# Setting constants of q and k on GpSimd instead of ScalarE, and loading the square-root table first, at the start of a gated attention kernel

## The chip, the core and the metric

The kernel runs on one core of one Trainium2 chip. The metric is the device time of one execution in microseconds. Three runs of the kernel before gave 3406.14 us as their median (3406.01 to 3406.58).

## What is computed

All data are float32. `x` has shape (2, 2048, 256). The reference, cut to what matters:

```
x = L0_attn_x
xn = layernorm(x)
s  = attn(xn)            # 16 heads of 16, over all 2048 tokens, with a spatial bias on a
                         # 256 x 256 corner of the scores; then W_proj, + b_proj, + layernorm(xn)*gamma+beta
g  = silu(ffn(xn))       # two layers: windowed attention with rotary positions, then a gated MLP
out = x + s * g

attn: qkv = xn @ W_qkv.T;  a = softmax(q @ k.T * hd**-0.5 + bias);  (a @ v) @ W_proj.T
```

The change lies in the first attention, `attn`, and there in its beginning.

## The kernel before

**Stages.** `global_attention` computes `s` in units of (batch element, group of 4 heads, 512 queries). In each it first finds the largest score of every query (`max_piece`, L364 on VectorE over L361's products), then forms the scores again with the maximum taken off (L397), their exponentials (L403 on ScalarE) and the sums with v (L416). `ffn_branch` follows. The change and the prediction concern the first 130 us or so, before the exponentials begin.

**The beginning.** x of batch element 0 is loaded in four chunks of 512 tokens (L226, four DMAs of 512 KB on SyncE's queue). For each chunk VectorE takes mean and variance (L212, L213), ScalarE takes the root (L234), VectorE the reciprocal and a shift (L235, L237), ScalarE scales the chunk in four pieces (L244), TensorE transposes it (L257) and ScalarE copies it to `xA` (L258). Then TensorE projects it to k and q (L293) and v (L327). k and q go by way of DRAM (L300 out, L308 back), because each head of 16 rows has to stand in a strip of 32 rows. `both` interleaves the lists of such steps of neighbouring chunks; this order is written out by hand, and every engine executes its own list in order. `spatial_bias` is interleaved later: ScalarE L100, L101, VectorE L102, ScalarE L103, three times.

**Constant places.** In the strip of 32 rows of a head, row 16 of `kT` holds ones and row 16 of `qT` takes the negative maximum later (`augment`); the other rows above 15 do not matter as long as those of `qT` are zero. `v` holds a one beside each head's 16 columns. There are two buffers of each, for alternating groups. `set_rest(i)` sets buffer i whole, before the DMAs of L308 write the 16 rows of each head: `kT` from `ones_col`, a column with a one in row 16 of each strip of 32, and `qT` from a zero column, both on ScalarE; `v` by a memset on GpSimd. It is called once at the head of the step lists and once for buffer 1 after the four chunks, ahead of the bias.

**What sets the order.** Up to `tc.manual_schedule()` a scheduler decides the order of an engine's instructions from the dependences; behind it the order is the program's. DMAs of SyncE's and ScalarE's queues take eight completion semaphores in rotation, in scheduler order. If the semaphore that a DMA is to take is still out, the DMA's issue waits until the earlier user has landed, and the queue behind it waits too. In the built program this gives, for the first DMAs (SyncE's in brackets): vecs 0, (x chunk 0) 1, b2 2, ones_col 3, wk 4, (x chunk 1) 5, wk 6, wq 7, (x chunk 2) 0, wq 1, wv 2, (x chunk 3) 3, wv 4, gam 5, bet 6, bpr 7. So x chunk 2 waits for vecs, x chunk 3 for ones_col, the second wv for the first wk, gam for x chunk 1, bet for the second wk, bpr for the first wq. ScalarE's DMA issues stand ahead of its first compute instruction.

The weights wk, wq, wv arrive padded (L161) and are packed on GpSimd (L164), each in two halves. `wp` is loaded by sixteen DMAs on GpSimd's own queue (L195).

Of the kernel before, what the change touches and what calls it, by code (L numbers as in the profile page):

```python
# [11 lines left out]
F32 = mybir.dt.float32  # L12
AF = mybir.ActivationFunctionType
ALU = mybir.AluOpType
AX = mybir.AxisListType
PSUM = bass.MemoryType.PSUM

B, N, D = 2, 2048, 256
P = 128
NT = N // P  # L20
# [6 lines left out]
NG, GH, HD, HP = 4, 4, 16, 32  # L27
NPR, PH = 2, 8
VW = HD + 1
VALL = (PH - 1) * VW + HP  # L30
# [10 lines left out]
def gated_recurrent_kernel(ctx: ExitStack, tc: tile.TileContext, t: dict, out: bass.AP):  # L41
# [31 lines left out]

    s_all = [s_pool.tile([P, NT, D], F32, tag=f"s{b}", name=f"s{b}") for b in range(B)]
    global_attention(tc, t, xA, s_all, s_out, ident, eps_t, x_ch, early)
    ffn_branch(tc, t, xA, s_out, weights, ident, eps_t, mean_w, vecs, b2_row, x_ch, out_ch)

# [59 lines left out]
def global_attention(tc, t, xA, s_all, s_out, ident, eps_t, x_ch, early):  # L137
# [9 lines left out]
    nc = tc.nc  # L147
    with ExitStack() as ctx:
        cp = ctx.enter_context(tc.tile_pool(name="ga_c", bufs=1))
        p2 = ctx.enter_context(tc.tile_pool(name="ga_2", bufs=2))  # L150
        psr = ctx.enter_context(tc.tile_pool(name="ps_r", bufs=1, space=PSUM))

        ones_col = cp.tile([P, 1], F32, name="ones_col")
        nc.scalar.dma_start(ones_col, t["ones"][:, 2 * P :])

        w, padded = {}, {}
        for n in ("wk", "wq", "wv"):
# [4 lines left out]
                padded[n, k] = x  # L162
        for n, k in padded:
            nc.gpsimd.tensor_copy(w[n][:, k].rearrange("p (h d) -> p h d", d=HD), padded[n, k][:, :, :HD])  # L164

        qTs = [cp.tile([P, N], F32, name=f"qT{i}") for i in range(2)]
        kTs = [cp.tile([P, N], F32, name=f"kT{i}") for i in range(2)]
        vs = [cp.tile([P, NT, VALL], F32, name=f"v{i}") for i in range(2)]
        zero = xA[0][:, 0, 0:1]

        def set_rest(i):
            nc.scalar.copy(kTs[i], ones_col.to_broadcast([P, N]))
            nc.scalar.copy(qTs[i], zero.to_broadcast([P, N]))
            nc.gpsimd.memset(vs[i], 1.0)

        dram = ctx.enter_context(tc.tile_pool(name="qk_d", bufs=1, space=bass.MemoryType.DRAM))
        qk_d = {}
# [170 lines left out]
        def max_piece(j):  # L348
            n, at = divmod(taken[j], TPC * NCH)
            if n >= len(units):  # L350
                return
            taken[j] += 1
            i, c = divmod(at, NCH) if n else divmod(at, TPC)[::-1]
            b, g, qc = units[n]
            qT, kT, _ = qkv[b * NG + g]
            if n not in mxs:
                mxs[n] = p2.tile([P, TPC * GH, NCH], F32, tag="mx", name=f"mx_{n}")
            rows = slice(j * HP, (j + 1) * HP)
            ps = bank(f"pm_{n}_{i}_{c}_{j}", ring="p")
            q0 = qc * CH + i * P  # L360
            nc.tensor.matmul(  # L361
                ps, qT[rows, q0 : q0 + P], kT[rows, c * CH : (c + 1) * CH], start=True, stop=True
            )
            nc.vector.tensor_reduce(mxs[n][:, i * GH + j, c : c + 1], ps, AX.X, ALU.max)  # L364
            if all(x >= (n + 1) * TPC * NCH for x in taken):
                nc.vector.tensor_reduce(negm[n % 2][:, :, HD : HD + 1], mxs[n], AX.X, ALU.max, negate=True)
                others.insert(0, lambda: augment(n))
# [122 lines left out]
        def both(a, b):  # L490

            n = max(len(a), len(b))
            for i in range(n):
                for x in (a, b):
                    for f in x[i * len(x) // n : (i + 1) * len(x) // n]:
                        f()
# [2 lines left out]
        turns = [firsts[c][0][3:] + firsts[c][1] for c in range(NCH)]  # L499
        preps = [first_preps(c) for c in range(NCH)]  # L500
        maxima = [[(lambda j=j: max_piece(j)) for _ in range(TPC) for j in range(GH)] for _ in range(NCH + 1)]
        set_rest(0)
        both(stat[0], [])
        both(turns[0], stat[1])
        both(preps[0] + turns[1], stat[2])
        both(preps[1] + turns[2], stat[3])
        both(maxima[0], preps[2] + turns[3])
        both(maxima[1], preps[3])
        set_rest(1)
        rest = [lambda: next(sb) for _ in range(4)] + prep[3 * NCH :]  # L510
        both(maxima[2] + maxima[3], rest[:-4])
        both(maxima[4][: LEAD * GH], [lambda: others.pop(0)()] + rest[-4:])
# [689 lines left out]
```

## Time and profile before

| | |
|---|---|
| median of three runs | 3406.14 us |
| the profiled execution's own time | 3405.59 us |
| its span, first to last instruction | 3403.8 us |
| mean granted TensorE clock | 0.987 |
| GpSimd: first / last packing copy of the weights | 9.72 / 15.59 us |
| GpSimd: the sixteen wp issues | 16.93 to 24.93 us |
| GpSimd: two memsets of v | 24.92 to about 29.0 us |
| first L361 of the maxima | 43.63 us |
| first exponential's table load | 133.95 us |

The profile shows one execution. A line of its timeline gives start and length in us, engine, line of the kernel, operation, result<-operands, how many were merged, and in brackets how long the engine stood idle before and what released it. ACTq, SPq and POOLq are the instruction queues' DMA issues, PEld is TensorE's weight load. In the 40 slices a digit is the busy share in tenths.

### The profile page before, as it was taken

The numbers are of one execution on the slowest core, as the hardware profiler recorded it, in microseconds if no ns is written. First come the engines' busy times: TensorE is split into PE (matmuls) and PEld (weight loads), VectorE is DVE, ScalarE is ACT, GpSimd is POOL, SyncE is SP. The second block draws the span as 40 slices with busy tenths as digits, with TensorE's granted clock in tenths as the row PEclk, the third lists the DMA queues.
The fourth block names the chain that finished last, engine by engine and source line by source line (L and its number), as shares of the span: only waits on it lengthen the run. The fifth ranks groups of instructions, "written<-read, shape, count | busy, mean of one in ns | idle before, by whom it ended". The sixth has DMA issues, their size and how long they took to land. (4 is left out here: it accounts for less than half of the span.)

```text
span 3403.8 us, 55360 instructions
## 1 busy us (share of the span) xinstructions
PE 3325.0 (98%) x21280; PEld 1631.7 (48%) x21280; DVE 2314.9 (68%) x4978; ACT 2092.9 (61%) x4237; POOL 1105.2 (32%) x949
## 2 busy tenths in 40 slices
PE   6999999999999999999999799999999999999999
PEld 3444444444444444444444355555555555666565
DVE  3798889877777787787775366666666666665642
ACT  3477676667776677767677576555555555555542
POOL 2012111111111111111111455555555555655631
PEclk8899999999999999999999899999999999999999
DMA  2100000000000100000000100000000000000001
GB/s 93 51 1 6 21 1 14 14 14 14 7 18 21 46 14 1 4 10 1 1 7 7 62 9 1 7 1 7 1 25 8 1 17 25 10 19 19 20 19 49
DMA packets 39768, 56.78 MB, mean 17 GB/s; under 512 B 8830, under 2 KB 24274, under 8 KB 39506
## 3 DMA queue, kind: packets, MB, share of 16 engines
q1 hardware_dynamic: 37266, 50.88, 4.7%
q8 instruction: 168, 2.75, 0.3%
q10 hardware_dynamic: 1728, 2.12, 0.2%
q14 instruction: 94, 0.77, 0.1%
q0 software_dynamic: 512, 0.26, 0.0%
HBM read 36.45 MB, written 16.78 MB: 16 GB/s over the span
## 5 line engine op out<-in xcount | busy, mean ns | idle before, releaser
L364 DVE TENSOR_REDUCE mx<-pm 128x1 f32<-128x512 f32 x2048 | 1272.2, 682 | 357.1 <-PE ps L397 311.7
L403 ACT ACTIVATE e<-ps 128x512 f32<-128x512 f32 x2048 | 1069.7, 602 | 258.2 <-PE ps L397 179.0
L361 PE MATMUL pm<-kT,qT 32*128 32x512 f32 x4096 | 1166.2, 626 | 3.6 <-DVE mx L364 3.6
L397 PE MATMUL ps<-qa,kT 32*128 32x512 f32 x4096 | 1109.6, 625 | 14.1 <-ACT e L403 14.1
L427 POOL TENSOR_TENSOR o<-o,part 128x512 f32<-128x512 f32 x224 | 284.3, 1269 | 1449.6 <-ACT part L426 1439.3
L361 PEld LDWEIGHTS pm<-kT,qT 32*128 32x128 f32 x4096 | 486.7, 185 | 375.3 <-DVE mx L364 262.6
L397 PEld LDWEIGHTS ps<-qa,kT 32*128 32x128 f32 x4096 | 442.1, 184 | 212.1 <-ACT e L403 142.5
L416 PE MATMUL po<-e,v 128*32 128x512 f32 x4096 | 497.5, 604 | 1.7 <-DVE mx L364 1.7
L721 PE MATMUL pp<-weights,xA 128*128 128x512 f32 x768 | 361.6, 606 | 0.8 <-DVE s L471 0.8
L937 PE MATMUL pg<-hc,weights 128*128 128x512 f32 (+1 forms) x768 | 357.6, 596 | 1.1 <-DVE hc L918 1.1
L743 POOL TENSOR_TENSOR rot<-rot,swp 128x512 f32<-128x512 f32 x128 | 166.9, 1304 | 515.6 <-DVE swp L740 504.0
L416 PEld LDWEIGHTS po<-e,v 128*32 128x32 f32 x4096 | 107.7, 109 | 353.4 <-DVE mx L364 183.9
L426 ACT COPY part<-po 128x512 f32<-128x512 f32 x224 | 131.4, 586 | 225.2 <-PE po L416 224.6
L811 ACT ACTIVATE sm<-sm,wmx 128x256 f32<-128x256 f32 (+1 forms) x512 | 249.3, 488 | 5.3 <-DVE wmx L803 4.5
L742 ACT ACTIVATE sqq<-pp 128x512 f32<-128x512 f32 x128 | 76.5, 598 | 262.5 <-DVE swp L740 254.1
L752 POOL TENSOR_TENSOR rn<-rn,mhalf 128x8 f32<-128x8 f32 x128 | 210.9, 1648 | 82.3 <-DVE rn L751 77.0
L825 POOL TENSOR_TENSOR sm<-sm,wls 128x512 f32<-128x512 f32 (+1 forms) x224 | 223.1, 1028 | 12.1 <-DVE wls L817 12.1
L937 PEld LDWEIGHTS pg<-hc,weights 128*128 128x128 f32 (+1 forms) x768 | 128.4, 178 | 156.2 <-issue 139.3
L721 PEld LDWEIGHTS pp<-weights,xA 128*128 128x128 f32 x768 | 136.6, 192 | 130.8 <-issue 122.6
L803 DVE CUSTOM_DVE_ANT_0 sm<-ps,mask 128x256 f32<-128x256 f32 (+1 forms) x512 | 181.2, 409 | 1.1 <-PE ps L790 1.0
L771 DVE COPY xT<-pt 128x512 f32<-128x512 f32 x64 | 44.2, 691 | 157.6 <-PE pt L765 157.5
L946 DVE SCALAR_TENSOR_TENSOR u<-pg,vecs,gl 128x512 f32<-128x512 f32 x96 | 70.4, 733 | 114.8 <-PE pg L937 101.4
(152 smaller groups left out, 3530.3 us busy)
## 6 DMA issues: line engine op xcount, KB each, us to landing
s<-in_x_dram SPq DMA_DIRECT2D x8, 512.0 KB, 5.0
qk_wk<-stage_wk SPq DMA_DIRECT2D x16, 256.0 KB, 2.0
kT<-qk_wk SPq DMA_DIRECT2D x128, 32.0 KB, 1.8
qk_wq<-stage_wq SPq DMA_DIRECT2D x16, 256.0 KB, 2.0
qT<-qk_wq SPq DMA_DIRECT2D x128, 32.0 KB, 1.8
s_out<-s SPq DMA_DIRECT2D x8, 512.0 KB, 2.7
s<-s_out SPq DMA_DIRECT2D x16, 256.0 KB, 3.5
x<-in_x_dram SPq DMA_DIRECT2D x16, 256.0 KB, 3.4
```

Of the source, the lines that this page charges most:

```text
L361: nc.tensor.matmul(ps, qT[rows, q0 : q0 + P], kT[rows, c * CH : (c + 1) * CH], start=True, stop=True)
L364: nc.vector.tensor_reduce(mxs[n][:, i * GH + j, c : c + 1], ps, AX.X, ALU.max)
L397: nc.tensor.matmul(ps, kT[rows, kt * P : (kt + 1) * P], qas[n][rows, :], start=True, stop=True)
L403: nc.scalar.activation(e, ps, AF.Exp)
L416: nc.tensor.matmul(pos[n][j * HP : (j + 1) * HP, :], v[:, kt, (r + j) * VW : (r + j) * VW + HP], es.pop((n, kt, j)), start=(kt % 2 == 0), ...
L427: nc.gpsimd.tensor_add(os[n], os[n], part)
L721: nc.tensor.matmul(ps, xA[b][:, k, at : at + P], W["qkv"][:, k, n * INNER : (n + 1) * INNER], start=(k == 0), stop=(k == 1),)
L752: nc.gpsimd.tensor_tensor(rn, rn, mhalf, ALU.pow)
L803: nc.vector.tensor_tensor_reduce(sm[:, x, lo:], pss[r][:, x, lo:], mask[:, lo:], -1.0, 3e38, ALU.add, ALU.min, mx[:, hb, r, x : x + 1],)
L811: nc.scalar.activation(sm[:, x, lo:], sm[:, x, lo:], AF.Exp, scale=-1.0, bias=mx[:, hb, r, x : x + 1], accum_out=ls[:, hb, r, x : x + 1],)
L825: nc.gpsimd.tensor_mul(sm, sm, ls[:, hb, r, :, None].to_broadcast([P, 2, 2 * P - lo]))
L937: nc.tensor.matmul(ps[:mw], W["1"][:, k, at : at + mw], hc[:, k, :], start=(k == 0), stop=(k == 1))
```

## The change

The column of ones is no longer loaded. It is the sum of four columns (16, 48, 80, 112) of the identity matrix, which lies in SBUF already, taken on VectorE. A root of a single constant on ScalarE makes the square-root table the first one that is loaded. `qT` and `kT` of both buffers are set on GpSimd, those of buffer 0 ahead of the packing of the weights. `v` of buffer 0 is set behind that packing.

```diff
         ones_col = cp.tile([P, 1], F32, name="ones_col")
-        nc.scalar.dma_start(ones_col, t["ones"][:, 2 * P :])
+        nc.vector.tensor_reduce(ones_col, ident[:, HD::HP], AX.X, ALU.add)
+        root_table = cp.tile([P, 1], F32, name="root_table")
+        nc.scalar.activation(root_table, eps_t, AF.Sqrt)
+
+        qTs = [cp.tile([P, N], F32, name=f"qT{i}") for i in range(2)]
+        kTs = [cp.tile([P, N], F32, name=f"kT{i}") for i in range(2)]
+        vs = [cp.tile([P, NT, VALL], F32, name=f"v{i}") for i in range(2)]
+        nc.gpsimd.memset(qTs[0], 0.0)
+        nc.gpsimd.tensor_copy(kTs[0], ones_col.to_broadcast([P, N]))
...
         for n, k in padded:
             nc.gpsimd.tensor_copy(w[n][:, k].rearrange("p (h d) -> p h d", d=HD), padded[n, k][:, :, :HD])
-
-        qTs = [cp.tile([P, N], F32, name=f"qT{i}") for i in range(2)]
-        kTs = [cp.tile([P, N], F32, name=f"kT{i}") for i in range(2)]
-        vs = [cp.tile([P, NT, VALL], F32, name=f"v{i}") for i in range(2)]
-        zero = xA[0][:, 0, 0:1]
-
-        def set_rest(i):
-            nc.scalar.copy(kTs[i], ones_col.to_broadcast([P, N]))
-            nc.scalar.copy(qTs[i], zero.to_broadcast([P, N]))
-            nc.gpsimd.memset(vs[i], 1.0)
+        nc.gpsimd.memset(vs[0], 1.0)
+
+        def set_rest():
+            nc.gpsimd.tensor_copy(kTs[1], ones_col.to_broadcast([P, N]))
+            nc.gpsimd.memset(qTs[1], 0.0)
+            nc.gpsimd.memset(vs[1], 1.0)
...
-        set_rest(0)
         both(stat[0], [])
...
-        set_rest(1)
+        set_rest()
```

In the built program after, the rotation reads: vecs 0, (x chunk 0) 1, b2 2, (x chunk 1) 3, wk 4, (x chunk 2) 5, wk 6, wq 7, (x chunk 3) 0, wq 1, wv 2, wv 3, gam 4, bet 5, bpr 6. The order of the instructions is otherwise the same on every engine, apart from the instructions that the diff moves: ScalarE has the table load and the new root behind b2's issue and ahead of wk's; VectorE has the sum behind the statistics of chunk 0; GpSimd has qT's memset, the mask's two selects and kT's copy ahead of the packing, v's memset behind it, and the second set behind the sixteen wp issues.

## The prediction

> **What bounds the kernel now.** I read the page first. TensorE is busy 98% of the span; of the 40 slices of 85 us two are under full, one in the middle (7) and the first (6), where the whole change lies. A gain or loss there reaches the end only as a shift of everything behind it.
>
> ```profile
> span 3403.8 us, 55360 instructions
> PE 3325.0 (98%) x21280; PEld 1631.7 (48%) x21280; DVE 2314.9 (68%) x4978; ACT 2092.9 (61%) x4237; POOL 1105.2 (32%) x949
> PE   6999999999999999999999799999999999999999
> ```
>
> Then the timeline of ScalarE (start, length, instruction), from which the change takes work:
>
> ```profile
> 1.76 0.52 ACTq L154 DMA_DIRECT2D ones_col<-in_ones_dram  x1
> 2.31 1.15 ACTq L161 DMA_DIRECT2D wk<-in_wk_dram  x2
> 3.50 1.79 ACTq L161 DMA_DIRECT2D wq<-in_wq_dram  x2
> 8.36 1.66 ACTq L161 DMA_DIRECT2D wv<-in_wv_dram  x2
> 10.06 0.45 ACTq L182 DMA_DIRECT2D gam<-in_ln_gamma_dram  x1
> 10.55 0.44 ACTq L184 DMA_DIRECT2D bet<-in_ln_beta_dram  x1
> 11.24 0.33 ACTq L186 DMA_DIRECT2D bpr<-in_b_proj_dram  x1
> 11.61 1.28 ACT L172 ACT_TABLE_LOAD   x1 [11.61 <-DMA wq<-in_wq_dram]
> 12.90 1.90 ACT L172 COPY kT<-ones_col 128x2048 f32<-128x2048 f32 x1
> 14.70 1.89 ACT L173 COPY qT<-xA 128x2048 f32<-128x2048 f32 x1
> 16.61 1.28 ACT L234 ACT_TABLE_LOAD   x1
> 17.91 0.30 ACT L234 ACTIVATE rs<-mv,eps_t 128x4 f32<-128x4 f32 x1
> ...
> 83.40 1.90 ACT L172 COPY kT<-ones_col 128x2048 f32<-128x2048 f32 x1
> 85.20 1.90 ACT L173 COPY qT<-xA 128x2048 f32<-128x2048 f32 x1
> 87.00 0.52 ACT L100 ACTIVATE bias<-cb,cp 128x256 f32<-128x256 f32 x1
> ```
>
> ScalarE issues DMAs up to 11.57, then fills 11.61 to 17.91 without a hole: load, two copies, load. The root at 17.91 heads a chain in which each step waits for the one before: VectorE's reciprocal (18.24), ScalarE's scaling (18.65), TensorE's transposes (19.35), the projections (22.02). The statistics it needs end on VectorE at 7.1. So **the first root is the late step**, and the question is when it can start after the change. That is set by the DMA issues ahead of it, so I read SyncE's waits and the landing of x last:
>
> ```profile
> SPq L226 <- DMA ones_col<-in_ones_dram: 4.7, 1, 4.7
> SPq L300 <- DMA s<-in_x_dram: 4.5, 1, 4.5
> SPq L226 <- DMA vecs<-in_vecs_dram: 2.4, 1, 2.4
> DMA to landing us min/median/max: 7.7/8.8/9.9
> ```
>
> The third and fourth chunks of x are held back by vecs and ones_col, with which they have nothing to do. The built program explains it: SyncE's and ScalarE's DMAs take eight completion semaphores in rotation, and one whose semaphore is still out waits for the earlier user. The second chunk lands at 1.2 + 7.7 = 8.9, the third at 4.1 + 9.9 = 14.0.
>
> **The change part by part.**
>
> *Away from ScalarE's head:* L172's load and both copies, and the second load moves. At most 17.91 - 11.61 = 6.3 us. The Trainium skill ("ScalarE: Activation LUTs", What ACT_TABLE_LOAD costs) puts about 1.38 us of drain on top of a load, 2.66 us each; two loads would be 5.3 us. Here the copy ends at 16.59, the load begins at 16.61 and the root follows 0.02 us after it: no drain, 2 x 1.28 = 2.6 us. The rows decide.
>
> *What then ends last ahead of the root:* the place of ones_col in the rotation goes, and all later DMAs move up by one. In the built program the second wv now waits for x's second chunk, gam for the first wk, bet for **x's third chunk**, bpr for the second wk. In turn the third chunk waits for nothing (issue about 1.7 instead of 4.1) and the fourth only for vecs (4.1 instead of 9.2). So up to 512 KB of x go ahead of the weights that bpr waits for. The stretch table gives 296 GB/s in 5 to 10 us and 355 in 10 to 15, with the DMA engines busy 0.93 and 1.03: full. At 355 GB/s, 512 KB are 1.5 us.
> - Served in order of issue: the second wk lands at 3.0 + 7.4 = 10.4 before, 11.9 after; x's third chunk at about 8.9 + 1.5 = 10.4. The issue of bpr ends at 11.9 + 0.33; the root starts at 12.3. Gain 17.91 - 12.3 = **5.6 us**.
> - Bound above: weights not displaced, third chunk early. bet at 10.5, bpr at 11.0, root at 11.3: 6.6 us.
> - Bound below: the third chunk lands at 14.0 as before. bet 0.44, bpr 0.33, gaps 0.1: root at 14.9, 3.0 us.
>
> I take the first, because wk, wk, wq landed in order of issue at 9.7, 10.4, 11.2. Against it: the third x, issued before the second wq, landed after it (14.0 against 12.4), though it is twice as large. Here a rule speaks against the change: the skill ("DMA: Bandwidth & Descriptors", Queues, rings and completion order) says that each DMA engine goes round between the queue rows it has work for. By it an earlier place in SyncE's queue buys x little, and the sum is the lower bound, 3.0; by order of issue it is 5.6.
>
> *New on ScalarE before the weights:* a load (1.28, row L234) and a root of one column (0.30, same row), less the ones_col issue (0.52). If the DMA issues wait for both, the first wk goes out at 1.73 + 1.6 = 3.3 instead of 2.3; if not, at 1.8. Cover: 1.5 MB of x, queued before it and not through before about 10. No cost; without that cover up to 1.0 us.
>
> *GpSimd before the weights:* qT's memset. Between negm's 512 (0.49) and v's 2416 (4.18 / 2 = 2.09) that is 1.8, at 2.1 to 3.9. Then kT's copy, behind VectorE's new ones_col, itself queued behind the first chunk's statistics (7.1). The reduction is 0.2 (nearest: the 0.18 reciprocal; VectorE waited 11.1 us at that place). The copy: nearest row is POOL COPY 128x256, 0.40 us; 8 x 0.40 = 3.2 above, the memset's 1.8 below; I take 2.6, so 7.3 to 9.9. Queued behind it are the weight copies, whose first load lands at 9.7 to 11.2. Cost nothing; TensorE wants wk only at 12.3 + 4.1 = 16.4 (as 22.02 follows 17.91). The skill advises against elementwise work on GpSimd ("GPSIMD Engine Reference", Performance versus the Vector engine: 4.5 us for a two-input add of 2048); by that price the copy ends at 11.8, still before TensorE's need.
>
> *GpSimd after the weights:* v0's memset (2.1) moves ahead of negm and of the sixteen wp issues (8.0 us), then kT1, qT1, v1: 2.6 + 1.8 + 2.1. v0 is done at about 18.5 and read at 29.33 - 5.6; wp lands by 30 and is first read at 439.9; cp's memset moves from 29.0 to about 35, its DMA comes at 83. Nothing. kT's first fetch (28.43 - 5.6) now also waits for the copy of 9.9: nothing.
>
> *At 83 us:* the copies of 83.40 and 85.20 go, and L100 starts 3.6 us sooner. But the add that needs it stands on VectorE behind six reductions that run from 83.97 to 87.65, and began at 87.96 after waiting 0.31 us. So 0.3 us of the 3.6, between 0 and 0.4; the second add waited 0.1.
>
> **Sum:** 5.6 + 0.3 = 5.9 us. The profiled execution took 3405.59 (span 3403.8 and 1.8 around it), so 3399.7; it lies 0.55 below the median, and the forecast on the median is 3406.14 - 5.9 = **3400.2 us**, -0.17%. Differences under 0.2% (6.8 us) I count as no change, about what a measurement of this kernel can tell.
>
> **A spread that no edit pays for:** the granted clock is 0.75 in 43 to 84 us, 0.65 in 84 to 94, 0.96 in 94 to 130. The wk projection takes 3.8 us in the half-clock windows (45.6, 69.0, 93.4) and 2.0 outside (104.2). A shift can move one in or out: 1.8 us either way. Four runs within 1.0 us say that it seldom adds up.
>
> **Rivals.**
> - *The wait moves to x's third chunk.* Root at 14.9, gain 3.0 + 0.3: 3402.8. For it the round of queues and the 14.0 landing; against it the earlier issue. 0.22.
> - *The weights are not displaced* (also for want of ones_col's 128 rows of 4 bytes): root at 11.3, 6.6 + 0.3: 3399.2. For it, x has 1.5 MB behind each other either way; against it, DMA engines at 0.93 and over. 0.18.
> - *Slower: GpSimd becomes the bound.* One place, kT's copy with its repeated source ahead of the weight copies. It starts at 7.3 and decides once it ends after about 15.4 (16.4 less the two wk copies), from 8 us on. To end over 6.8 us slower than before it must take about 8 + 5.9 + 6.8 = 21 us, 8 times my value: 3413. For it, GpSimd's L752 takes 1648 ns for 8 elements; against it, its plain copies take 0.40 for 256. 0.05.
> - *The load is not saved* (a second one stays before the root): the built program has one load up to the exponentials. Would cost 1.3: 3401.5, inside the range.
>
> **Numbers.** The forecast's own case 0.55. Faster by over 0.2%: three quarters of the undisplaced case (0.135) and 0.4 of the likeliest, where the clock adds 0.9 us or more (0.22): 0.355. Slower: 0.05. The rest, 0.595, within 0.2%. The range 3397.4 to 3403.4 takes the likeliest with 1.8 us either way, the undisplaced with 1.8 us of gain, the moved wait with 0.6 of loss; outside lie the slow case and the tails, under 0.15.
>
> **What would show it.** Right: the first root near 12.3, ended by bpr's issue, which waits for the second wk; first transposes near 13.7; VectorE's first bias add with no wait. Wrong: bet issued at 14 behind x (first rival); bpr by 11 (second); wk's copies on GpSimd released by GpSimd's own copy, not by a DMA (third). Wrong too if the shift at the first root and the one at 130 us differ by over 2 us: then the clock's windows decided.

## The result and the profile after

| | before | after |
|---|---|---|
| median of the comparison (22 runs each) | 3403.97 us | 3397.97 us |
| ratio, 95% interval | | 0.9983, 0.9977 to 0.999 |
| the profiled execution's own time / its span | 3405.59 / 3403.8 us | 3398.29 / 3396.2 us |
| first root on ScalarE starts | 17.91 us | 13.64 us |

The change is worth 6.0 us of the medians, 3.4 to 7.8 by the interval; the forecast was 5.9. (The forecast of 3400.2 us started from a median of 3406.14 for the kernel before; here it has 3403.97, so the forecast of the time itself is 2.2 us too high.) The sum came out right, but not all of its terms, and not for its whole reason: the first root gained 4.3 us, not 5.6, another 1.15 us is gained at 232 us, where the forecast had nothing, and what is left goes with TensorE's clock, as the runs below show.

The page of the kernel after: the span, the busy times and TensorE's slices. As before, two slices of 40 are under full.

```profile
span 3396.2 us, 55360 instructions
PE 3322.9 (98%) x21280; PEld 1632.9 (48%) x21280; DVE 2314.3 (68%) x4979; ACT 2083.7 (61%) x4233; POOL 1111.0 (33%) x953
PE   7999999999999999999999799999999999999999
```

ScalarE's timeline after (start, length, engine, line, operation):

```profile
1.76 1.28 ACT L157 ACT_TABLE_LOAD   x1 [1.76 <-issue]
1.83 1.27 ACTq L170 DMA_DIRECT2D wk<-in_wk_dram  x2
3.06 0.20 ACT L157 ACTIVATE root_table<-eps_t 128x1 f32<-128x1 f32 x1
3.13 2.66 ACTq L170 DMA_DIRECT2D wq<-in_wq_dram  x2
8.35 1.07 ACTq L170 DMA_DIRECT2D wv<-in_wv_dram  x2
11.03 0.34 ACTq L187 DMA_DIRECT2D gam<-in_ln_gamma_dram  x1
12.77 0.34 ACTq L189 DMA_DIRECT2D bet<-in_ln_beta_dram  x1
13.15 0.45 ACTq L191 DMA_DIRECT2D bpr<-in_b_proj_dram  x1
13.64 0.30 ACT L239 ACTIVATE rs<-mv,eps_t 128x4 f32<-128x4 f32 x1 [10.38 <-DMA wq<-in_wq_dram]
```

The 6.3 us between the last issue and the root are gone: bpr's issue ends at 13.60, the root starts at 13.64. But the issues themselves end 2.0 us later than before (11.57). The page names wq as the releaser of the root, but its first half was in place at 13.11, before bpr went out; what held ScalarE is seen in the starts of the issues. gam goes out at 11.03, bet 1.4 us after gam's issue ended. By the rotation bet waits for x's third chunk, and that chunk's semaphore is set at 12.75; bpr waits for the second wk, which the trace has at 12.01, so that bpr is held by nothing but bet. The two views of x (SyncE's waits, then the spans from issue to landing) show that its third chunk was no longer held back, and still was slow:

```profile
SPq L231 <- DMA vecs<-in_vecs_dram: 1.7, 1, 1.7
```

```profile
0.73 3.63 SPq L231 DMA_DIRECT2D s<-in_x_dram  x4
```

The four issues of x are over by 4.4 us (9.5 before), the ones_col wait is gone. The third chunk, issued some 2.4 us earlier than before, landed only 1.3 us earlier (12.75 against 14.06).

On GpSimd after, the cost of the new work and what the packing waits for:

```profile
2.05 1.80 POOL L162 MEMSET qT<- 128x2048 f32 x1
...
7.09 1.89 POOL L163 COPY kT<-ones_col 128x2048 f32<-128x2048 f32 x1 [2.75 <-DVE ones_col L155]
11.06 0.40 POOL L173 COPY wk<-wk 128x256 f32<-128x256 f32 x1 [2.08 <-DMA wk<-in_wk_dram]
```

The copy is done at 9.0, and GpSimd then stands idle for 2.08 us until wk lands: it is nobody's bound. At 83 us VectorE's first bias add, which waited 0.31 us before (first line), follows the reductions without a wait after (second view), while ScalarE now waits for the centres' DMA (third):

```profile
87.96 0.42 DVE L102 TENSOR_TENSOR bias<-bias,dy 128x256 f32<-128x256 f32 x1 [0.31 <-ACT dy L101]
```

```profile
79.78 3.68 DVE L369 TENSOR_REDUCE mx<-pm 128x1 f32<-128x512 f32 x6 [1.86 <-PE pm L366]
83.38 0.42 DVE L102 TENSOR_TENSOR bias<-bias,dy 128x256 f32<-128x256 f32 x1
```

```profile
82.22 0.53 ACT L100 ACTIVATE bias<-cb,cp 128x256 f32<-128x256 f32 x1 [2.91 <-DMA cp<-in_centers_dram]
```

**Where the time came from.** I pair every VectorE instruction of the two traces and call the difference of their starts the lead. It is 4.27 us at the first root, 4.19 at 84 us, 4.59 at 90, 4.38 at 130. Up to there it is the beginning's. At 200 us it is still 4.47, at 250 us 5.60, with the granted clock at 1.00 in both kernels. The stretch tables (stretch, length, busy time and count by engine, then the granted clock, the DMA share and GB/s), before and then after, and what VectorE and GpSimd do at that place, before and then after:

```profile
200.00:250.00 50.00, 48.94 (x375) 20.83 (x366) 45.22 (x86) 34.89 (x66) 10.06 (x9) 1.00 0.01 1
```

```profile
200.00:250.00 50.00, 50.00 (x376) 21.85 (x376) 45.57 (x88) 35.87 (x68) 9.06 (x9) 1.00 0.00 1
```

```profile
231.01 0.48 DVE L281 SCALAR_TENSOR_TENSOR s<-s,mvs,gam 128x256 f32<-128x256 f32 x1
...
231.84 1.26 POOL L427 TENSOR_TENSOR o<-o,part 128x512 f32<-128x512 f32 x1 [1.19 <-ACT part L426]
231.94 1.44 DVE L282 SCALAR_TENSOR_TENSOR s<-s,rss,bet 128x256 f32<-128x256 f32 x1 [0.46 <-DVE s L281]
```

```profile
226.56 0.48 DVE L286 SCALAR_TENSOR_TENSOR s<-s,mvs,gam 128x256 f32<-128x256 f32 x1
...
227.14 0.48 DVE L287 SCALAR_TENSOR_TENSOR s<-s,rss,bet 128x256 f32<-128x256 f32 x1
...
227.38 1.37 POOL L432 TENSOR_TENSOR o<-o,part 128x512 f32<-128x512 f32 x1 [1.19 <-ACT part L431]
```

The VectorE step is L282, L287 after, the second line of a layernorm; GpSimd adds up a part of the attention's result (L427, L432). In the kernel before, the step begins 0.93 us after the start of the one ahead of it, in the kernel after 0.58 us, so that before GpSimd's addition begins first. VectorE's step then takes 1.44 us instead of 0.48, and TensorE stands idle for 1.06 us of this stretch. All four builds of this document that load the column of ones show the 1.44 us (1.437 to 1.445), and none of the ten that take it from the identity matrix does. So this gain of 1.15 us is the change's as well. What holds VectorE's step back by the 0.35 us the traces do not show.

Behind 350 us the lead wanders: 8.4 at 600 us, 4.9 at 1300, 1.5 at 1600, 7.65 at the end. Most of this is when TensorE's granted clock falls to 0.5, for 3.4, 6.8 or 10.2 us at a time; smaller steps, up to 0.5 us, stand beside it. The stretch tables again, before and then after:

```profile
350.00:370.00 20.00, 18.72 (x109) 6.23 (x105) 16.01 (x35) 11.12 (x21) 2.53 (x2) 0.83 0.33 86
...
1850.00:1865.00 15.00, 14.66 (x76) 5.25 (x72) 0.00 (x0) 10.27 (x21) 2.53 (x2) 0.77 0.01 2
```

```profile
350.00:370.00 20.00, 19.33 (x129) 8.35 (x126) 19.63 (x46) 14.60 (x28) 1.27 (x1) 1.00 0.25 70
1020.00:1030.00 10.00, 9.60 (x49) 3.32 (x50) 8.51 (x19) 5.67 (x11) 0.00 (x0) 0.83 0.14 34
```

Before has its half clock at 360 and 1855 us (0.83 over 20 us, 0.77 over 15), after has full clock at 360 and a short one at 1025. Behind 150 us the half-clock time adds up to 44.2 us before and 37.4 after. (A last piece, which begins some 6 us before the end in every build, is left out here and below.)

### The profile page after: what moved, and what is told of

It is laid out like the page before. It is cut to its first block, busy times and chain, and to the rows that moved or that the text cites. A ratio compares the mean times of both kernels' runs of the same rounds, so it can differ in the third digit from the quotient of the medians.

```text
span 3396.2 us, 55360 instructions
## 1 busy us (share of the span) xinstructions
PE 3322.9 (98%) x21280; PEld 1632.9 (48%) x21280; DVE 2314.3 (68%) x4979; ACT 2083.7 (61%) x4233; POOL 1111.0 (33%) x953
## 5 line engine op out<-in xcount | busy, mean ns | idle before, releaser
L432 POOL TENSOR_TENSOR o<-o,part 128x512 f32<-128x512 f32 x224 | 283.9, 1268 | 1446.7 <-ACT part L431 1436.4
```

The lines of the kernel that those rows point to most:

```text
L432: nc.gpsimd.tensor_add(os[n], os[n], part)
```

## The experiments

**Theory L** (lead; the expectations of the last runs call it D): the edits act only on the beginning. They free 6.3 us of ScalarE, lose 2.0 because the early x pushes the last landings back, and what remains, 4.3 to 4.4 us of lead at 130 us, is what they are worth; the rest of any difference is half-clock time met later. **Rival W** (the forecast's own case): wk ends the wait, x does not matter. **Rival P** (places): the new addresses of q, k and v in SBUF make the later stages faster. **Rival E** (engine): GpSimd in ScalarE's place changes the later stages.

### The ones from the identity matrix, alone

```diff
 # kernel before
-        nc.scalar.dma_start(ones_col, t["ones"][:, 2 * P :])
+        nc.vector.tensor_reduce(ones_col, ident[:, HD::HP], AX.X, ALU.add)
```

> The kernel before with one edit: the column of ones comes from the identity matrix, so ones_col's DMA and its place in the rotation of semaphores are gone; loads of tables and copies on ScalarE stay. Theory 1 (the last constants wait for x's third chunk): bet is issued near 12.8 us, ScalarE's first table load starts near 13.6 instead of 11.6, the first root near 19.9 instead of 17.9; 2.0 us slower, on top of a scatter of some 3 us between single runs. Theory 2 (the constants wait for the displaced second wk, as forecast): loads start near 12.3, root near 18.6, 0.7 us slower. Theory 3 (the rotation costs nothing): root at 17.9, no change.

Measured: 3404.45 us (before 3404.21), ratio 0.9994 (0.9988 to 1.0001): no difference clear of noise. ScalarE's timeline:

```profile
11.56 0.34 ACTq L184 DMA_DIRECT2D bet<-in_ln_beta_dram  x1
12.67 0.33 ACTq L186 DMA_DIRECT2D bpr<-in_b_proj_dram  x1
13.04 1.28 ACT L172 ACT_TABLE_LOAD   x1 [13.04 <-DMA wq<-in_wq_dram]
...
19.33 0.30 ACT L234 ACTIVATE rs<-mv,eps_t 128x4 f32<-128x4 f32 x1
```

Taking away a 128 x 1 load makes the root 1.4 us later, between what the two theories said. In this build's rotation bet waits for the second wk, whose semaphore is set at 11.54, and bpr for the first wq, set at 12.65 (11.22 in the kernel before). x's third chunk, for which no issue of ScalarE waits here, is in at 12.92. From issue to landing, wq's first half and then x:

```profile
DMA to landing us min/median/max: 9.4/9.4/9.4
```

```profile
DMA to landing us min/median/max: 4.3/8.0/11.2
```

So here the weights end the wait, put back by x: wq by 1.4 us, and wk near the forecast's 11.9. The chunk comes 2.5 us behind the forecast's 10.4. The lead is -1.4 us at the root and -0.5 at 130 us; the clock rose sooner (5.1 us after the first matmul, not 6.2), which was not separated. At 232 us this build, alone of the edits made one by one to the kernel before, gains the 1.15 us: its lead is +0.64 at 250 us.

```profile
232.10 0.48 DVE L282 SCALAR_TENSOR_TENSOR s<-s,rss,bet 128x256 f32<-128x256 f32 x1
```

### The change without the early root

```diff
 # kernel after
-        nc.scalar.activation(root_table, eps_t, AF.Sqrt)
```

> The changed kernel without the early root, so that the square-root table is loaded in front of the first real root. Theory 1: the DMA issues don't wait for the early load, the weights land as in the changed kernel, and the root moves from 13.6 to 14.9 us by the load's 1.28: 1.3 us of the gain. Rival: the early load held the weights up; without it they go out sooner and the root comes at 13.9 or before, so that the early root is worth 0.3 us or nothing.

Measured: 3397.33 us, ratio 0.9977 (0.9966 to 0.9988).

```profile
12.68 0.34 ACTq L189 DMA_DIRECT2D bpr<-in_b_proj_dram  x1
13.11 1.28 ACT L237 ACT_TABLE_LOAD   x1 [13.11 <-DMA wq<-in_wq_dram]
14.40 0.30 ACT L237 ACTIVATE rs<-mv,eps_t 128x4 f32<-128x4 f32 x1
```

The load is back on the path (1.28 us), but the root is only 0.76 later: bpr ends at 13.02 instead of 13.60, as here bpr, the last issue, waits for the first wq (set at 12.66), and in the changed kernel bet waits for the third chunk (12.75), with bpr still to issue. The lead is 3.45 at the root. The time does not resolve 0.8 us: it came out lower, not higher.

### The early root, alone

```diff
 # kernel before
+        root_table = cp.tile([P, 1], F32, name="root_table")
+        nc.scalar.activation(root_table, eps_t, AF.Sqrt)
```

> The kernel before with one part of the change alone: the root of eps first on ScalarE, so that the table is loaded at 1.76 us and neither of the two loads stands between the last constant's issue and the first root. Theory: 2 x 1.28 us off the path, less up to 0.55 us by which the issues end later: first root at 15.35 to 15.9 us (17.91 before), lead 2.0 to 2.6 us there and at 130 us; by theory D the time is 3400 to 3403, and the profile's span + lead follows its half-clock time. Rival (the root's table as a part has no worth, as the run of the changed kernel without it, 3397.3, would have it): root as before, 3404.

Measured: 3401.74 us (before 3404.45), ratio 0.9993 (0.9984 to 1.0001).

```profile
12.58 0.33 ACTq L188 DMA_DIRECT2D bpr<-in_b_proj_dram  x1
12.96 1.90 ACT L174 COPY kT<-ones_col 128x2048 f32<-128x2048 f32 x1 [9.14 <-DMA wq<-in_wq_dram]
14.76 1.89 ACT L175 COPY qT<-xA 128x2048 f32<-128x2048 f32 x1
16.56 0.29 ACT L236 ACTIVATE rs<-mv,eps_t 128x4 f32<-128x4 f32 x1
```

Both loads are off the path, yet the root is at 16.56, 1.35 us earlier and not 2.0 to 2.6: the expectation was wrong by the issues, which end at 12.91, 1.3 us later than before. The cause is again the rotation. The new instruction shifts the order in which the scheduler hands out semaphores, and in this build x's third chunk waits for nothing. It is in at 11.34; bpr waits for the second wk, set at 12.56, as rival W has it. So the four builds so far that let x's third chunk out early end their issues at 12.9 to 13.6, whichever edit did it; the kernel before, which holds it back, at 11.6. Which transfer is the last one waited for differs with the rotation.

### Gamma, beta and bias behind x on SyncE

```diff
 # kernel after
-        nc.scalar.dma_start(gam, t["ln_gamma"][None, :].to_broadcast([P, D]))   # bet, bpr likewise
...
             f[0].pop(0)()                                                       # the four x loads
+            nc.sync.dma_start(gam, t["ln_gamma"][None, :].to_broadcast([P, D])) # bet, bpr likewise
```

> The changed kernel, but gamma, beta and the projection bias are issued on SyncE behind the four x loads instead of on ScalarE between the weight loads and the first root. Theory L (the beginning acts on the time by the lead that it gives, and only by that): ScalarE then holds no issue behind the last weight load, whose own wait is for the first wk (9.2 us behind its issue at 1.83, so 11.0); the first root starts at about 11.4 instead of 13.64, the lead over the kernel before is about 6.5 us instead of 4.3, and the time is 2.2 us below the changed kernel's: about 3396 where the changed kernel is 3398. Rival (the weights end the wait all the same: the first projections, behind the root by 2.5 us, wait for wk's packing, which ends near 13): root at 11.4, but the first projection where it is now, the lead past 30 us stays at 4.3, time 3398.

Measured: 3396.26 us (before 3403.83), ratio 0.9975 (0.9966 to 0.9984).

```profile
8.23 3.38 ACTq L170 DMA_DIRECT2D wv<-in_wv_dram  x2
11.65 0.30 ACT L236 ACTIVATE rs<-mv,eps_t 128x4 f32<-128x4 f32 x1 [8.39 <-DMA wq<-in_wq_dram]
```

The root follows the second wv at 11.65, as expected (11.4). The lead is 6.26 us at the root and 6.1 at 130 us, so the 2 us that bet and bpr cost are real and reach TensorE; the first projection waits for no packing. The rival falls. The time is 1.7 us below the changed kernel's of the first comparison; the intervals overlap.

### The wv loads behind x on SyncE as well

```diff
 # kernel above; the packing of wv and the wp loads stand behind these lines
-                nc.scalar.dma_start(x, t[n][:, k].rearrange("p (h d) -> p h d", d=HP))   # for wv
+            nc.sync.dma_start(padded["wv", k], t["wv"][:, k].rearrange("p (h d) -> p h d", d=HP))
```

> As the run before it, and the two wv loads are issued on SyncE behind the x loads as well, their packing on GpSimd with them, the projection weights' loads behind it. Theory L: ScalarE's last issue is the second wq, which waits only for the first x chunk; the first root follows its data at about 7.5 us, lead 10 at the root; but the first projections need wk, whose second half lands near 12 and is packed by 12.9, so that the lead past 20 us is 9 at most and 6.5 to 7 if wk ends the wait; time 3393 to 3396. Rival (the total does not follow the early lead): the trace shows the lead, the time stays at 3397 to 3399.

Measured: 3390.79 us, ratio 0.9968 (0.9956 to 0.9979). It is the fastest version tried. First ScalarE, then TensorE:

```profile
7.22 0.30 ACT L234 ACTIVATE rs<-mv,eps_t 128x4 f32<-128x4 f32 x1 [3.95 <-DVE mv L213]
```

```profile
8.65 2.75 PE L257 MATMUL pt<-ident,s 128*128 128x128 f32 x8 [8.65 <-ACT s L244]
13.17 3.78 PE L293 MATMUL pp_wk<-xA,wk 128*128 128x512 f32 x4 [1.76 <-POOL wk L175]
```

Now the root is released by its own data, the variance, at 7.2 us; the early end of the chain is reached. What is late next is also seen: the wk projection waits 1.76 us for GpSimd's packing, and here kT's copy does stand in the way, for it ran from 10.88 to 12.77 (the sum of ones came late on VectorE) and the packing begins at 12.72. The lead is 10.7 us at the first root, 5.95 at 35 us and 13.5 at 130 us, more than expected. The early half-clock time is 27.2 us here and 40.9 before, which by the rate found below (0.35) would be about 5 us; against it, the clock rises 10.2 us after the first matmul here and 6.2 before. The two were not taken apart, so how much of the 13.5 us is the edit's is not shown.

### The first buffers on ScalarE, twice

```diff
 # kernel after
-        nc.gpsimd.memset(qTs[0], 0.0)
-        nc.gpsimd.tensor_copy(kTs[0], ones_col.to_broadcast([P, N]))
...
+        nc.scalar.copy(kTs[0], ones_col.to_broadcast([P, N]))
+        nc.scalar.copy(qTs[0], xA[0][:, 0, 0:1].to_broadcast([P, N]))
         both(stat[0], [])
```

> The changed kernel with kT and qT of buffer 0 set by ScalarE again, ahead of the first root. Theory 1: the two copies of 1.9 us stand between bpr's issue and the root: root at 13.6 + 3.7 = 17.3 us, 0.6 us ahead of the kernel before. Rival (the copies fit under the wait for the constants): they are queued behind the constants' issues, so they can't; root below 16 would show it.

Measured: 3398.68 us, ratio 0.9984 (0.9976 to 0.9992). The root is at 17.64, as expected (17.3): the two copies, 3.6 us beside each other, are the largest part of the gain. But the time says nearly as fast as the change itself, with a lead of 0.6 us at 130 us. This spoke against theory L, so the kernel was run once more.

> The changed kernel with the first buffers of q and k set on ScalarE, once more, beside the changed kernel itself on the same chip. Theory D: lead 0.3 at the root and 0.6 at 130 us again; whether the time is again near 3398.7 depends on its half-clock time behind 150 us (27.2 us in its profile so far): if that is a trait of the kernel, 3397 to 3400 again, single times close together; if it was chance, the median moves towards 3403.

Measured: 3403.10 us (before 3404.45), ratio 0.9987 (0.9976 to 0.9997); the root at 17.07. The single times lie in two groups with nothing between, five from 3392.9 to 3393.6 and seven from 3402.7 to 3405.3, where the first comparison had them between 3396.7 and 3399.5 but for one. The mean granted clock is 0.991 in the five, 0.987 or 0.988 in the seven; 0.001 is 6.8 us of half clock. The profiled run of the second is of the lower group. The stretch tables of the two profiles, first comparison and second:

```profile
55.00:80.00 25.00, 22.31 (x67) 8.25 (x66) 13.78 (x23) 4.92 (x9) 0.00 (x0) 0.73 0.10 34
```

```profile
55.00:80.00 25.00, 21.89 (x82) 9.03 (x82) 15.85 (x26) 4.29 (x8) 0.00 (x0) 0.86 0.15 44
```

One half-clock window is 13.7 us long in the first and 6.8 in the second, and TensorE gets through 82 matmuls in place of 67. The lead jumps from 1.6 to 4.6 us at that place, with the same instructions. So one program can differ by 10 us from run to run by its clock windows alone, and the first low median is no evidence against theory L.

### The second buffers on ScalarE, and on GpSimd alone

```diff
 # kernel after
-            nc.gpsimd.tensor_copy(kTs[1], ones_col.to_broadcast([P, N]))
-            nc.gpsimd.memset(qTs[1], 0.0)
+            nc.scalar.copy(kTs[1], ones_col.to_broadcast([P, N]))
+            nc.scalar.copy(qTs[1], xA[0][:, 0, 0:1].to_broadcast([P, N]))
```

> The changed kernel with kT and qT of buffer 1 set by ScalarE again, ahead of the bias. Theory 1: VectorE is busy with maxima meanwhile, so the lead over the kernel before at 130 us is between 4.0 and 4.4 us, as against 4.4 in the changed kernel. Rival (the 3.6 us of copies stand in the chain): lead near 0.8 us.

Measured: 3395.63 us, ratio 0.9974 (0.9963 to 0.9986). The wait is back ahead of VectorE's first bias add:

```profile
84.39 0.42 DVE L102 TENSOR_TENSOR bias<-bias,dy 128x256 f32<-128x256 f32 x1 [0.32 <-ACT dy L101]
```

Between 84 and 90 us the lead stays at 3.57, where the changed kernel goes from 4.19 to 4.59. The time lies below the changed kernel's (3397.97) all the same; the profile has 27.2 us of half clock behind 150 us, against 37.4. The other way round, the same part alone in the kernel before:

```diff
 # kernel before
-        set_rest(1)
+        nc.gpsimd.tensor_copy(kTs[1], ones_col.to_broadcast([P, N]))
+        nc.gpsimd.memset(qTs[1], 0.0)
+        nc.gpsimd.memset(vs[1], 1.0)
```

> The kernel before with one part of the change alone: the second buffers of q and k are set on GpSimd instead of ScalarE. Theory D (the edits give the lead that the trace shows at 130 us, and the rest of a difference in time is how many windows of half clock the run meets later; span + lead at 130 us is then the same for equal half-clock time): no lead at the root (17.9), 0.3 to 0.4 us from 90 us on, and span + lead = 3403.7 less about 0.4 us for every us of half clock below 44.2 behind 150 us. Median 3401 to 3405. Rival (GpSimd instead of ScalarE at that place is what lowers the number of windows): the profile has 37.4 us or less of half clock behind 150 us, and most single times lie at 3399 or below.

Measured: 3404.83 us (before 3404.45), ratio 1.0002 (0.9994 to 1.0011). The lead goes from 0.94 at 84 us to 1.33 at 90: 0.4 us. Half-clock time behind 150 us: 44.2 us, as before, so rival E falls. A lead of 0.56 us was there at the root already, with no edit ahead of it: the loads landed sooner on this chip (bpr's issue ends at 11.02). That is the scatter of a root's place from one profile to another; the changed kernel's head gave 13.1 to 13.6 in four profiles.

### Places in SBUF

```diff
 # kernel before: q, k, v ahead of the weights, as in the changed kernel
+        qTs = [cp.tile([P, N], F32, name=f"qT{i}") for i in range(2)]      # kTs, vs likewise
         w, padded = {}, {}
```

> The kernel before with one edit that moves no instruction: q, k and v are given their places in SBUF ahead of the weights, as in the changed kernel. Theory L (lead only): no lead at any place, time as the kernel before, 3404, ratio 1.000 within 0.0007. Rival P (the change of places in SBUF, not the lead, brings part of the 6 us, as it would explain that the changed kernel with buffer 0 set on ScalarE has a lead of 0.6 us and yet ran 5.5 us below): no lead up to 150 us, but 3 to 5 us less in the time, about 3400.

```diff
 # kernel after: the weights ahead of q, k, v, as in the kernel before
+        w = {n: cp.tile([P, 2, NPR * P], F32, name=n) for n in ("wk", "wq", "wv")}
         qTs = [cp.tile([P, N], F32, name=f"qT{i}") for i in range(2)]
```

> The changed kernel with one edit that moves no instruction: the weights are given their places in SBUF ahead of q, k and v, as in the kernel before. Theory L: lead 4.3 us at the first root and 4.4 at 130 us as in the changed kernel, time 3398 to 3400. Rival P (places): the same lead at the beginning, but only that much in the end, and the time 3 to 5 us above the changed kernel's, 3400 to 3402.

Measured: 3404.66 us, ratio 1.0003 (0.9995 to 1.0012), and 3397.25 us, ratio 0.9982 (0.9973 to 0.999). The leads at 130 us are -1.0 and 5.9, where none and 4.4 were expected: the roots came 0.2 us later and 0.5 us sooner than in the kernels that they copy, and the clock rose 7.1 and 5.2 us after the first matmul (6.2 and 6.3 there). The times are those of kernels with the same instructions, whatever the places. Rival P falls.

### The changed kernel once more

> The changed kernel once more, for its own spread on the chip of the other three. Theory D: first root 13.6 us, lead 4.3 to 4.5 at 130 us; with 37.4 us of half clock behind 150 us a span of 3396.2, with 27.2 us 3392.7; median 3396 to 3399.

Measured: 3396.19 us (before 3404.45), ratio 0.9976 (0.9966 to 0.9986). Root 13.53, lead 4.30 at 150 us, 37.4 us of half clock, span 3396.4: as expected.

### All profiled runs together

If theory L holds, span plus lead at 150 us must be one number for equal half-clock time, and fall evenly with it. The lead at 250 us stands beside it, as it takes in the step at 232 us. The half-clock time is the sum of the pieces behind 150 us in which the trace's record of the granted clock has 0.5.

| kernel | span | half clock, us | lead at 150 us | span + lead at 150 | lead at 250 us | span + lead at 250 |
|---|---|---|---|---|---|---|
| before | 3403.8 | 44.2 | 0 | 3403.8 | 0.0 | 3403.8 |
| ones alone | 3404.1 | 44.2 | -0.5 | 3403.6 | 0.6 | 3404.7 |
| second buffers alone | 3402.8 | 44.2 | 1.2 | 3404.0 | 1.2 | 3404.0 |
| after | 3396.2 | 37.4 | 4.4 | 3400.6 | 5.6 | 3401.8 |
| after, once more | 3396.4 | 37.4 | 4.3 | 3400.7 | 5.5 | 3401.9 |
| after, no early root | 3397.0 | 37.4 | 3.6 | 3400.6 | 4.8 | 3401.8 |
| after, places of before | 3394.6 | 37.4 | 5.9 | 3400.5 | 7.1 | 3401.7 |
| constants on SyncE | 3394.6 | 37.4 | 6.1 | 3400.7 | 7.4 | 3402.0 |
| wv on SyncE too | 3386.8 | 37.4 | 13.5 | 3400.3 | 14.8 | 3401.6 |
| before, places of after | 3401.8 | 34.0 | -1.0 | 3400.8 | -1.0 | 3400.8 |
| early root alone | 3398.7 | 34.0 | 1.9 | 3400.6 | 1.6 | 3400.3 |
| after, second buffers on ScalarE | 3393.6 | 27.2 | 3.5 | 3397.1 | 4.7 | 3398.3 |
| after, first buffers on ScalarE | 3396.5 | 27.2 | 0.6 | 3397.1 | 1.9 | 3398.4 |
| the same, once more | 3391.5 | 27.2 | 5.1 | 3396.6 | 6.3 | 3397.8 |

With the lead at 150 us the sum is 3403.6 to 3404.0 at 44.2 us of half clock, 3400.3 to 3400.8 at both 34.0 and 37.4, and 3396.6 to 3397.1 at 27.2: nearly one number for each amount, but two amounts share one. With the lead at 250 us it falls evenly: 3404.2, 3401.8, 3400.6 and 3398.2 on the mean. So a microsecond of lead is a microsecond of time, over leads from -1.0 to 14.8, whatever made the lead (in the last row it is mostly early clock); and a microsecond of half clock costs about 0.35 (3404.2 - 3398.2 = 6.0 for 17.0). Theory L stands for the beginning and for the clock, but its claim that the edits act only on the beginning falls: the step at 232 us comes with the ones from the identity matrix. The spans of the two kernels' first profiles differ by 7.6 us: 4.4 of lead from the beginning, 1.15 at 232 us, and some 2 of half clock.

## Why the prediction was right, and where it was not

- **What bounds the beginning.** Right. The first root was the late step; from before to after, its 4.27 us reached TensorE whole.
- **Away from ScalarE's head, 6.3 us, loads at 1.28 without a drain.** Right: after bpr's issue 0.04 us pass to the root, 6.34 before. No run shows a drain behind a load: the early root's instruction starts 0.02 us after its load ends (1.76 + 1.28, 3.06), and without the early root the first root starts 0.01 us after it. The Trainium skill's 1.38 us ("ScalarE: Activation LUTs", What ACT_TABLE_LOAD costs) is not met here.
- **"At 355 GB/s, 512 KB are 1.5 us": the failed term.** The prediction put x's third chunk at 10.4 and wk last at 11.9, hence the root at 12.3. wk came at 12.01, as forecast, so that x did put the weights back. The chunk came at 12.75, so the wait had moved to it, as the first rival said, with bet and bpr still to issue behind it. It did not land as that rival had it, at 14.0, but some two thirds of the way from 10.4 (2.35 of 3.6). Neither order of issue nor the skill's plain round of queues ("DMA: Bandwidth & Descriptors", Queues, rings and completion order) gives the number; a sum of 12.75 + 0.85 would have. The term was 5.6 and measured 4.3. With bet and bpr out of the way the root went to 11.65, which shows the place. The three other builds that let the chunk out early have another rotation, and there a weight half ended the wait (12.56 to 12.66).
- **The early load.** The prediction left open whether the DMA issues wait for it. They do not: wk is issued at 1.83, inside the load of 1.76 to 3.04.
- **GpSimd.** The copy costed at 2.6 took 1.89, the memset 1.80 as forecast. Its cover held: 2.08 us of idle stood behind it. When the root was brought to 7.2 us, the same copy ended the wait, so this rival is the next bound, not a far one.
- **At 83 us, 0.3 of 3.6 us.** Right: 0.4 us with and without the part, in three traces.
- **The clock, "seldom adds up".** Too small. It was put at 1.8 us either way, from four close runs. Behind 150 us it made some 2 us between the two profiles, and single times of one kernel lie up to 12 us apart (3397.9 to 3410.2 for the kernel before in one comparison).
- **A gain that the sum did not have.** The forecast looked no further than 130 us and put nothing behind it. The 1.15 us at 232 us come with the ones from the identity matrix. The forecast's 5.9 against 6.0 is so partly luck: the change's own gain is about 5.5 us (5.60 and 5.51 of lead at 250 us in its two profiles, inside the interval of 3.4 to 7.8), and it comes near the sum because 1.3 us less at the root met 1.15 us that nobody had forecast. Some 0.5 us of the medians is left to the half-clock windows.

**What stays open.** What picks the windows. They stand on a grid: the one at 1025 us begins 1003.5 us behind the first rise of the clock in the changed kernel, and so in six other builds that have a window there, and 1003.5 is 294 times 3.413; in two more it begins at 292 and 295 times (996.7 and 1006.9). The Trainium skill ("TensorE: Matmul & The Clock Gate", What's actually happening) describes an activity window of that length which runs free of the kernel's start. The runs agree: the clock rises 5.0 to 7.1 us after the first matmul in all builds but the last of those with constants on SyncE. So a shift, or chance alone, moves the kernel's pauses against the grid, and could turn a window to half clock or spare it; that is argued, as no run shifted the kernel and nothing else. Why the kernel before meets 44.2 us in its profile and the changed kernel 37.4 in both of its own, no run here settles. It is not these profiles alone: of the changed kernel's 30 timed runs 29 have a mean granted clock of 0.988 and one 0.989; of 100 runs of the kernel before on three chips 58 have 0.986 or 0.987, the others 0.988 to 0.990. How much of it would come again stays open: beyond the change's 5.5 us the medians show 0.5 in the first comparison (6.0) and 2.8 in the second (8.3). Open too is what holds VectorE back by 0.35 us at 232 us; the builds without that wait have one VectorE instruction more (the sum) and one DMA less, and no run parted the two. Why the chunk took 11 us from issue to landing was not tried apart either, as with a smaller chunk or another queue order.

## What to carry to other kernels

Removing a tiny load can make the first step later (by 1.4 us here): where queues take completion semaphores in rotation, it changes which transfer each later issue waits for, and which large transfers compete. After an edit at a kernel's beginning, look at the issue that ends last ahead of the first step that matters, and move issues that nobody needs yet behind it or to another queue; here both moves together took the time from 3403.83 to 3390.79 us, though the clock has a part in that. For a change of a thousandth, measure the lead in the trace, instruction by instruction, not only behind the edited stage but along the whole kernel. Where it steps, compare the granted clock of both traces: here one step came with no change of the clock, and every build with the same edit had it.

## What the runs showed of the hardware that was not expected

- A DMA issue on ScalarE goes on while its table is being loaded (issue at 1.83, load 1.76 to 3.04).
- TensorE's granted clock falls to 0.5 late in a kernel that keeps TensorE busy at 98%, in five to eight windows of 3.4, 6.8 or 10.2 us behind 150 us, 27 to 44 us in all; a microsecond of it costs about 0.35 us, less than the half that the rate alone would take, and one program meets different sets of windows in different runs.
- After the start, x's third chunk of 512 KB took 11.2 us from issue to landing when issued at 1.76 us (with the ones from the identity alone), among 1.5 MB of other x and 1.5 MB of weights, and 9.9 when it was held back to 4.1; with the early root alone, issued at 1.76 as well, it took 9.6.
- A VectorE step of 128 x 256 that began 0.10 us after an addition of 128 x 512 on GpSimd took 1.44 us; begun 0.24 us ahead of that addition it took 0.48, and GpSimd's took 1.37 instead of 1.26 (builds before and after, at 232 us).
